# A hybrid two-layer network on one core: another form of the power in the scan step, and the long convolution's transposes and projections issued one group later

## The chip, the core and the metric

The kernel runs on one core of a Trainium2 chip. The core has a matrix engine (TensorE, called PE in the profile), a vector engine (VectorE, DVE), an activation engine (ScalarE, ACT), a general-purpose engine (GpSimd, POOL) and an engine that mostly issues transfers (SyncE, SP). Each has its own queue of instructions; they synchronise through semaphores. The metric is the device time of one execution in microseconds.

## The reference, cut to what matters

The network is a stack of sublayers, each added to x. Two of them are touched. The first is a recurrent scan over 2048 positions of a complex state h (256 channels by 16 modes, for two sequences):

```python
def step(h, inp):
    x_t, dt_t, B_t, C_t, xr_t = inp
    h_carrier = h.mean(axis=1)
    T = jnp.cos((c_phase(xr_t) - c_phase(h_carrier)) / 2.0) ** 2
    alpha = jnp.exp(dt_t[..., None] * A_neg)
    expo = 1.0 + (1.0 - alpha) * KAPPA * (1.0 - T[:, None, :])
    mag, ph = (c_mag(h), c_phase(h))
    cmag = jnp.minimum(jnp.exp(expo * jnp.log(mag + 1e-08)), 10.0)
    h = from_polar(cmag, ph)
    Bx = B_t[:, None, :, :] * (dt_t * x_t)[:, :, None, None]
    h = h + Bx
    h = from_polar(jnp.tanh(c_mag(h)), c_phase(h))
    y_t = jnp.einsum('bnc,bdnc->bd', C_t, h)
    return (h, y_t)
```

So each step raises the magnitude of h to a power that depends on the angle between h's mean over the channels and a given direction, adds an input, and squashes the magnitude with tanh. Step t needs all of step t-1. The second is a sublayer with a short causal convolution of four taps, a Silu, a long causal convolution with 1024 taps for each of 512 channels, a gate and a projection:

```python
xz = jnp.einsum('bld,ed->bel', hidden_states, W_in)
x, z = jnp.split(xz, 2, axis=1)
...
x = _silu(xc)
...
n = 2 * Lq
x_f = jnp.fft.rfft(x, n=n)
k_f = jnp.fft.rfft(k_ssm, n=n)
y = jnp.fft.irfft(x_f * k_f[None], n=n)[..., :Lq]
y = y + x * D_skip[None, :, None]
y = y * _silu(z)
return jnp.einsum('bhl,dh->bld', y, W_out)
```

## The kernel before

**The scan.** The state of a step lies as 128 partitions (two sequences, 16 modes, four quarters of the channels) by two planes (real and imaginary) by 64 channels, in hist. A hardware loop of four turns runs over 32 groups of 16 steps, 2048 steps in all. Inside it the order of every engine's instructions is the order in which the code is written (manual_schedule). In `step` (L388 to L480) the mean over the channels comes first: the last step's sums hs go through eight small matmuls (L400) into two PSUM tiles hc and hd, of which ACT reads hc and DVE reads hd. ACT makes n2c, the squared length of the mean, from hc (L415), then its logarithm and ci, one over its length (L423, L424). DVE makes dot, its product with the given direction, from hd (L417). With lg, the logarithm of the magnitude with its small additions, the power is split in two factors: ea = exp(om lg) (L429, L433) and fac = exp(ci lg dot ng) (L431, L440), where ng and om are prepared from alpha a group ahead by `decay` (L373 to L377). The unit vector p = h times il (L435, L436) is multiplied by ea (L438) and by fac (L443), and bx, the input, is added (L445). The rest of the step makes the magnitude m (L458 to L460), its inverse ir (L462), e = exp(-2m) (L463) and sg = 1/(1+e) (L465, L467), and forms the new h in two DVE operations with sums (L474), each followed by an instruction that reads the sum out into hs. In between and behind them DVE makes t2, the new squared magnitude, out of e2 and s2 of ACT (L479), and y1 (L480), from which the next step's logarithms l2 and lh start (L405, L409). Two hooks, act_gap and dve_gap, place work of other steps: the next step's bx (L381) and a part of `decay` behind fac on ACT; outputs and tables on DVE. `project` (L485) is the output product of the step before, on PE behind the mean. `load` (L355) issues the transfers of the next group on SP.

**The long convolution** (sublayer c). The 512 channels are four blocks e of 128. For each block and each of its 16 groups g of channels, `convolve` (L1156) issues 288 pairs of weight load and matmul on PE against Toeplitz windows of the taps, which `kernels` (L1097) loads three groups ahead at most, 2 x 1216 KB for a group, on SP and ACT. `produce(e, ch)` makes a chunk of 512 positions of the next block: a matmul (L1119), a copy on ACT (L1125), four taps on DVE (L1128, L1130), Silu on ACT into c_xs (L1132), and then at once the transpose on PE (ps_t, L1140) and its copy into the ring c_x on DVE (L1144). `finish(e, ch)` takes a chunk of the block before: it loads yc and xs back on POOL (L1176, L1177), makes the gate by a matmul and Silu (L1181, L1183), multiplies on DVE (L1184, L1185) and at once projects on PE (ps_o, L1189) and adds to x (L1193). Only PE's order is the written one here; the other engines' order comes from the scheduler. Behind the convolution of each even group a finish stands, behind that of each odd group a produce. Ahead of the first block stand eight produces, behind the last one eight finishes.

Of the kernel before, what the change touches and what calls it, by code (L numbers as in the profile page):

```python
# [17 lines left out]
AF = mybir.ActivationFunctionType  # L18
# [5 lines left out]
P = 128  # L24
# [39 lines left out]
class Kernel:  # L64
# [189 lines left out]
    def scan(self, y, dtd, dxd, tabd):  # L254
# [9 lines left out]
        with ExitStack() as c:  # L264
# [51 lines left out]
            with nc.allow_non_contiguous_dma(reason="short vectors"):  # L316
# [15 lines left out]
            t2 = [new(cp, [P, J], f"t2{j}") for j in range(2)]  # L332
            y1 = [new(cp, [P, J], f"y1{j}") for j in range(2)]
            bx = [new(cp, [P, 2, J], f"bx{j}") for j in range(2)]
            tg = [[new(cp, sh, f"{n}{j}") for n, sh in (
                ("tc", [P, 6, TG]), ("ng", [P, TG, J]), ("om", [P, TG, J]), ("dx", [P, TG, J]),
# [6 lines left out]
            V.tensor_tensor(t2[1], first[:, 1], first[:, 1], ALU.mult)  # L343
            V.tensor_tensor(y1[1], first[:, 0], first[:, 0], ALU.mult)
            V.tensor_tensor(t2[1], t2[1], y1[1], ALU.add)
            V.scalar_tensor_tensor(y1[1], first[:, 0], 2.0 * SMALL, t2[1], ALU.mult, ALU.add)
# [3 lines left out]
            def load(t0, j):  # L350
                tc_, ng, om, dx, cs = tg[j]
# [11 lines left out]
            def picked(j, k2):  # L363
                V.tensor_tensor(
                    tg[j][4][:, k2], tg[j][0][:, 2 + k2, :].unsqueeze(2).to_broadcast([P, TG, 8]),
                    pick.rearrange("p b r -> p (b r)").unsqueeze(1).to_broadcast([P, TG, 8]), ALU.mult,
                )

            def decay(j, s0, n, what):

                ng, om = tg[j][1][:, s0 : s0 + n], tg[j][2][:, s0 : s0 + n]
                if what == 0:
                    A.activation(ng, ng, AF.Exp, scale=aneg)  # L373
                elif what == 1:
                    A.activation(om, ng, AF.Identity, scale=-0.125, bias=0.625)
                else:
                    A.activation(ng, ng, AF.Identity, scale=0.125, bias=-0.125)  # L377

            def drive(j, k, k2, o):

                A.activation(  # L381
                    bx[o][:, k2], tg[j][3][:, k], AF.Identity, scale=tg[j][0][:, k2, k : k + 1],
                    bias=0.0 if k2 else SMALL,
                )

            w = lambda sh, name: new(wp, [P, *sh], name)
            wa = lambda name: new(pa, [P, J], name)

            def step(k, g, before, act_gap, dve_gap):

                tc_, ng, om, dx, cs = tg[g]
                ng, om = ng[:, k], om[:, k]
# [4 lines left out]
                hc, hd = new(pp, [P, 2], "hc"), new(pp, [P, 2], "hd")  # L397
# [23 lines left out]
                ln, ci, il = wa("lr")[:, 0:1], w([1], "ci"), w([J], "il")  # L421
                A.activation(il, lh, AF.Exp, scale=-0.5)
                A.activation(ln, n2c, AF.Ln, bias=1e-18)  # L423
                A.activation(ci, ln, AF.Exp, scale=-0.5)  # L424
# [8 lines left out]
                A.activation(ea, a, AF.Exp)  # L433
                p = w([2, J], "p")
                V.scalar_tensor_tensor(p[:, 0], h[:, 0], SMALL, il, ALU.add, ALU.mult)  # L435
                V.tensor_tensor(p[:, 1], h[:, 1], il, ALU.mult)  # L436
                for k2 in range(2):
                    V.tensor_tensor(p[:, k2], p[:, k2], ea, ALU.mult)  # L438
                fac = w([J], "fac")
                A.activation(fac, ngd, AF.Exp, scale=ci)  # L440
# [16 lines left out]
                m, lr = wa("m"), wa("lr")  # L457
                A.activation(m, m2, AF.Ln)  # L458
                A.activation(lr, r1, AF.Ln)
                A.activation(m, m, AF.Exp, scale=0.5)  # L460
# [1204 lines left out]
```

## Time and profile before

| | us |
|---|---|
| median of 3 runs | 14502.04 (14501.18 to 14502.08) |
| the profiled execution | 14511.68 |
| its span in the profile | 14510.0 |
| DVE busy | 10157.4 (70%) |
| ACT busy | 8884.8 (61%) |
| PE busy, weight loads apart | 5471.0 (38%) |
| POOL busy | 419.8 (3%) |
| mean granted PE clock | 0.616 of full speed |

By stage, from the windows of the trace:

| stretch, us | DVE busy | ACT busy | PE busy | granted PE clock | GB/s of DMA |
|---|---|---|---|---|---|
| 0 to 300, ahead of the scan | 213.90 | 108.84 | 155.26 | 0.73 | 51 |
| 5000 to 9000, in the scan | 3303.19 | 3090.32 | 769.64 | 0.50 | 15 |
| 11500 to 12000, in the long convolution | 83.56 | 30.11 | 297.54 | 0.80 | 164 |

How to read it: a group of the profile is one line, engine, operation and shape, with its count, its busy time and the mean duration of one in nanoseconds; behind a bar stands the engine's idle time just ahead of it, and who ended it. A timeline row has the start, the duration and the instruction. The duration of an operation includes its latency; the next one on the same engine can start before it ends. "issue" means that the engine waited for nothing that the profile shows.

### The profile page before, as it was taken

What the parts mean: (1) busy time and instruction counts of PE and PEld (TensorE: products, weight loads), DVE (VectorE), ACT (ScalarE), POOL (GpSimd) and SP (SyncE); (2) the same over time, 40 slices, a digit from 0 to 9 for tenths busy, and PEclk for the clock granted to TensorE, in tenths of its full rate; (3) what the DMA queues carried; (4) which work ended last, traced back from release to release, by engine and by line L of the source; (5) the groups of instructions that cost most, each with busy time, mean ns of one, the idle gap of its engine ahead of it and who ended that gap; (6) DMA issues with size and microseconds to landing.
All of it is one profiled execution on the core that took longest, in us unless ns stands there. A gap on an engine that the chain in (4) does not pass through costs nothing. (4 is left out here: it accounts for less than half of the span.)

```text
span 14510.0 us, 276079 instructions
## 1 busy us (share of the span) xinstructions
PE 5471.0 (38%) x72424; PEld 3825.2 (26%) x72424; DVE 10157.4 (70%) x63112; ACT 8884.8 (61%) x47340; POOL 419.8 (3%) x496
## 2 busy tenths in 40 slices
PE   4111111111111111111111111111797555878889
PEld 1111111111111111111111111111454444544445
DVE  6888888888888888888888888888475111355552
ACT  3777777777777777777777777777162000134442
POOL 0000000000000000000000000000000000121110
PEclk6555555555555555555555555555697787989999
DMA  2000000000000000000000000000001666142210
GB/s 65 13 16 16 13 16 16 16 13 16 16 16 13 16 16 13 16 16 16 13 16 16 15 15 16 16 13 16 25 1 40 166 162 168 29 88 35 35 28 14
DMA packets 349072, 460.71 MB, mean 32 GB/s; under 512 B 204930, under 2 KB 244937, under 8 KB 346452
## 3 DMA queue, kind: packets, MB, share of 16 engines
q1 hardware_dynamic: 296276, 319.90, 9.8%
q10 hardware_dynamic: 36352, 88.61, 2.6%
q0 software_dynamic: 14848, 34.36, 0.8%
q8 instruction: 580, 9.50, 0.3%
q14 instruction: 1016, 8.32, 0.2%
HBM read 385.55 MB, written 52.46 MB: 30 GB/s over the span
## 5 line engine op out<-in xcount | busy, mean ns | idle before, releaser
L400 PE MATMUL hc<-hs,mean 128*32 128x2 f32 x16384 | 588.7, 200 | 7982.7 <-DVE y L480 7727.5
L400 PEld LDWEIGHTS hc<-hs,mean 128*32 128x32 f32 x16384 | 472.7, 140 | 8115.0 <-ACT l L405 8038.0
L470 DVE TENSOR_TENSOR p<-p,ir 128x64 f32<-128x64 f32 x4096 | 739.1, 222 | 1063.4 <-ACT ir L462 1063.4
L485 PE MATMUL yps<-cs,hist 128*64 128x8 f32 x8192 | 1225.3, 259 | 13.8 <-DVE hs L474 13.8
L458 ACT ACTIVATE m<-m 128x64 f32<-128x64 f32 x2048 | 466.2, 228 | 1233.0 <-DVE m L452 1233.0
L381 ACT ACTIVATE bx<-dx,tc 128x64 f32<-128x64 f32 x4098 | 1170.1, 333 | 0.0
L1489 ACT ACTIVATE d_p<-ps_e 128x512 f32<-128x512 f32 (+3 forms) x1280 | 599.6, 537 | 756.0 <-PE ps_o L1470 535.2
L485 PEld LDWEIGHTS yps<-cs,hist 128*64 128x64 f32 x8192 | 1033.5, 218 | 45.9 <-DVE hs L474 14.2
L405 ACT ACTIVATE l<-t 128x64 f32<-128x64 f32 x2048 | 466.2, 228 | 766.2 <-DVE t L479 766.1
L474 DVE CUSTOM_DVE_ANT_0 hist<-p,sg 128x64 f32<-128x64 f32 x4096 | 910.7, 222 | 26.9 <-ACT s L468 6.4
L411 DVE SCALAR_TENSOR_TENSOR lg<-ih,l 128x64 f32<-128x64 f32 x2048 | 454.3, 222 | 561.5 <-ACT ih L407 557.3
L443 DVE TENSOR_TENSOR p<-p,fac 128x64 f32<-128x64 f32 x4096 | 739.9, 222 | 16.7 <-DVE p L438 6.6
L438 DVE TENSOR_TENSOR p<-p,ea 128x64 f32<-128x64 f32 x4096 | 742.0, 222 | 6.0 <-DVE p L438 4.7
L472 DVE SCALAR_TENSOR_TENSOR p<-e,p 128x64 f32<-128x64 f32 x4096 | 739.8, 222 | 6.0 <-ACT sg L467 5.3
L445 DVE TENSOR_TENSOR p<-p,bx 128x64 f32<-128x64 f32 x4096 | 726.1, 219 | 1.4
L440 ACT ACTIVATE fac<-ngd,ci 128x64 f32<-128x64 f32 x2048 | 692.4, 338 | 6.3 <-DVE p L436 5.4
L400 PE MATMUL hd<-hs,mean 128*32 128x2 f32 x16384 | 603.9, 193 | 0.0
L1482 PE MATMUL ps_e<-d_qt,d_kt 128*128 128x512 f32 (+3 forms) x1280 | 556.5, 444 | 44.2 <-ACT d_p L1489 35.6
L431 DVE SCALAR_TENSOR_TENSOR ngd<-lg,dot,ng 128x64 f32<-128x64 f32 x2048 | 570.4, 279 | 0.9 <-DVE a L429 0.9
L1439 PE MATMUL ps_m<-d_kt,d_qt 128*128 128x512 f32 (+3 forms) x1280 | 500.2, 438 | 101.1 <-DVE d_part L1444 41.0
L400 PEld LDWEIGHTS hd<-hs,mean 128*32 128x32 f32 x16384 | 532.7, 157 | 0.0
L1156 PE MATMUL ps_c<-toep,c_x 64*32 64x128 f32 x18432 | 405.6, 335 | 316.3 <-issue 281.4
(429 smaller groups left out, 21285.6 us busy)
## 6 DMA issues: line engine op xcount, KB each, us to landing
toep<-in_C_krev ACTq DMA_DIRECT2D x64, 1216.0 KB, 13.3
toep<-in_C_krev SPq DMA_DIRECT2D x64, 1216.0 KB, 10.7
ng<-dtd SPq DMA_DIRECT2D x258, 256.0 KB, 3.6
dx<-dxd SPq DMA_DIRECT2D x258, 256.0 KB, 4.3
d_kt<-d_kd SPq DMA_DIRECT2D x128, 128.0 KB, 4.4
d_qt<-d_qd SPq DMA_DIRECT2D x128, 128.0 KB, 4.4
y<-ys SPq DMA_DIRECT2D x512, 8.0 KB, 1.9
c_xd<-c_xs POOLq DMA_DIRECT2D x32, 256.0 KB, 7.3
```

What stands on the lines that cost most here:

```text
L381: A.activation(bx[o][:, k2], tg[j][3][:, k], AF.Identity, scale=tg[j][0][:, k2, k : k + 1], bias=0.0 if k2 else SMALL,)
L400: nc.tensor.matmul(out[r : r + 32], mean[:, r : r + 32], hs[i], start=True, stop=True)
L431: V.scalar_tensor_tensor(ngd, lg, dot, ng, ALU.mult, ALU.mult)
L438: V.tensor_tensor(p[:, k2], p[:, k2], ea, ALU.mult)
L440: A.activation(fac, ngd, AF.Exp, scale=ci)
L443: V.tensor_tensor(p[:, k2], p[:, k2], fac, ALU.mult)
L445: V.tensor_tensor(p[:, k2], p[:, k2], bx[o][:, k2], ALU.add)
L470: V.tensor_tensor(p[:, k2], p[:, k2], ir, ALU.mult)
L472: V.scalar_tensor_tensor(p[:, k2], e, -1.0, p[:, k2], ALU.add, ALU.mult)
L474: V.tensor_tensor_reduce(out=hn[:, k2], in0=p[:, k2], in1=sg, scale=-1.0, scalar=0.0 if k2 else J * SMALL, op0=ALU.mult, op1=ALU.add, accu ...
L485: nc.tensor.matmul(yps[:, k, :], hist[g][:, k, k2], tg[g][4][:, k2, k], start=k2 == 0, stop=k2 == 1)
L1489: A.activation(pr[:, q0:], s[:, q0:], AF.Exp, scale=0.25)
```

## The change

In the scan the power is written otherwise. Before, |h|^expo = exp(om lg) exp(ng lg cos) times the unit vector. After, p = h ek fac with fac = exp(lg ng (cos - 1)), so that h itself takes the part of exponent one, and with ek an exponential of the small additions alone. The factor cos - 1 = ci dot - 1 is a new ACT operation on one column, c1, which then is the scale of fac. The carried values of a step are x (minus the magnitude, from e and sg), kc and dl (small additions) instead of t2 and y1; for them ACT makes rm, lb, k1 and k2c. om goes. The tiles hc and hd are made once ahead of the loop, and a matmul of one column with ci is written into hd after its reader. In the convolution the transpose is a function `turn`, called a group later than its produce, and the projection a function `project`, called a group later than its finish; in the prologue and at the end `later` holds them back by one chunk. With om's 8 KB of each partition free, the scheduler places the load of x (L575 before) ahead of the scan.

```diff
-            t2 = [new(cp, [P, J], f"t2{j}") for j in range(2)]
-            y1 = [new(cp, [P, J], f"y1{j}") for j in range(2)]
+            x, kc, dl = ([new(cp, [P, J], f"{n}{j}") for j in range(2)] for n in ("x", "kc", "dl"))
             bx = [new(cp, [P, 2, J], f"bx{j}") for j in range(2)]
             tg = [[new(cp, sh, f"{n}{j}") for n, sh in (
-                ("tc", [P, 6, TG]), ("ng", [P, TG, J]), ("om", [P, TG, J]), ("dx", [P, TG, J]),
+                ("tc", [P, 6, TG]), ("ng", [P, TG, J]), ("dx", [P, TG, J]),
                 ("cs", [P, 2, TG, 8]))] for j in range(2)]
...
-                hc, hd = new(pp, [P, 2], "hc"), new(pp, [P, 2], "hd")
                 for out in (hc, hd):
                     for r in range(0, P, 32):
                         nc.tensor.matmul(out[r : r + 32], mean[:, r : r + 32], hs[i], start=True, stop=True)
                 before()
 
-
-                l2 = wa("l2")
-                A.activation(l2, t2[i], AF.Ln, bias=MAG_EPS)
-                ih = w([J], "ih")
-                A.activation(ih, l2, AF.Exp, scale=-0.5)
-                lh = w([J], "lh")
-                A.activation(lh, y1[i], AF.Ln)
-                lg = w([J], "lg")
-                V.scalar_tensor_tensor(lg, ih, 2.0 * MAG_EPS, l2, ALU.mult, ALU.add)
+                lh, lg, kd = (w([J], n) for n in ("lh", "lg", "kd"))
+                A.activation(lh, x[i], AF.Ln, scale=-1.0)
 
 
                 sq, n2c = w([2], "sq"), w([1], "n2c")
@@ -418,26 +419,25 @@
                     out=junk, in0=hd, in1=tc_[:, 4:6, k], scale=1.0, scalar=0.0, op0=ALU.mult, op1=ALU.add,
                     accum_out=dot,
                 )
-                ln, ci, il = wa("lr")[:, 0:1], w([1], "ci"), w([J], "il")
-                A.activation(il, lh, AF.Exp, scale=-0.5)
+                V.scalar_tensor_tensor(kd, kc[i], 0.5, dl[i], ALU.mult, ALU.add)
+                V.scalar_tensor_tensor(lg, lh, 2.0, kc[i], ALU.mult, ALU.add)
+                ln, ci, c1, ek = wa("lr")[:, 0:1], w([1], "ci"), w([1], "c1"), w([J], "ek")
                 A.activation(ln, n2c, AF.Ln, bias=1e-18)
                 A.activation(ci, ln, AF.Exp, scale=-0.5)
-
-
-
-                a = w([J], "a")
-                V.tensor_tensor(a, om, lg, ALU.mult)
-                ngd = w([J], "ngd")
-                V.scalar_tensor_tensor(ngd, lg, dot, ng, ALU.mult, ALU.mult)
-                ea = w([J], "ea")
-                A.activation(ea, a, AF.Exp)
+                A.activation(ek, kd, AF.Exp)
+                A.activation(c1, ci, AF.Identity, scale=dot, bias=-1.0)
+
+
+                nc.tensor.matmul(hd[32:33, 0:1], ci, self.ident[:, 0:1], start=True, stop=True)
+
+
+                gl = w([J], "gl")
+                V.tensor_tensor(gl, lg, ng, ALU.mult)
                 p = w([2, J], "p")
-                V.scalar_tensor_tensor(p[:, 0], h[:, 0], SMALL, il, ALU.add, ALU.mult)
-                V.tensor_tensor(p[:, 1], h[:, 1], il, ALU.mult)
-                for k2 in range(2):
-                    V.tensor_tensor(p[:, k2], p[:, k2], ea, ALU.mult)
+                V.scalar_tensor_tensor(p[:, 0], h[:, 0], SMALL, ek, ALU.add, ALU.mult)
+                V.tensor_tensor(p[:, 1], h[:, 1], ek, ALU.mult)
                 fac = w([J], "fac")
-                A.activation(fac, ngd, AF.Exp, scale=ci)
+                A.activation(fac, gl, AF.Exp, scale=c1)
...
-                m, lr = wa("m"), wa("lr")
-                A.activation(m, m2, AF.Ln)
+
+
+                lm, m, lr = wa("lm"), wa("m"), wa("lr")
+                A.activation(lm, m2, AF.Ln)
                 A.activation(lr, r1, AF.Ln)
-                A.activation(m, m, AF.Exp, scale=0.5)
-                ir, e, sg, e2, s2 = (w([J], n) for n in ("ir", "e", "sg", "e2", "s2"))
+                A.activation(m, lm, AF.Exp, scale=0.5)
+                ir, e, sg, rm = (w([J], n) for n in ("ir", "e", "sg", "rm"))
                 A.activation(ir, lr, AF.Exp, scale=-0.5)
                 A.activation(e, m, AF.Exp, scale=-2.0)
+                A.activation(rm, lm, AF.Exp, scale=-1.0)
                 le = wa("m")
                 A.activation(le, e, AF.Ln, bias=1.0)
-                A.activation(e2, e, AF.Square, bias=-1.0)
                 A.activation(sg, le, AF.Exp, scale=-1.0)
-                A.activation(s2, le, AF.Exp, scale=-2.0)
+                lb, k1, k2c = wa("lb"), w([J], "k1"), w([J], "k2c")
+                A.activation(lb, m2, AF.Ln, bias=MAG_EPS)
+                A.activation(k1, rm, AF.Ln, scale=MAG_EPS, bias=1.0)
+                A.activation(k2c, lb, AF.Exp, scale=-0.5)
...
-                    if k2 == 0:
-                        V.tensor_tensor(t2[o], e2, s2, ALU.mult)
-                V.scalar_tensor_tensor(y1[o], hn[:, 0], 2.0 * SMALL, t2[o], ALU.mult, ALU.add)
+                V.scalar_tensor_tensor(x[o], e, -1.0, sg, ALU.add, ALU.mult)
+                V.scalar_tensor_tensor(dl[o], hn[:, 0], -SMALL, rm, ALU.mult, ALU.mult)
+                V.scalar_tensor_tensor(kc[o], k2c, 2.0 * MAG_EPS, k1, ALU.mult, ALU.add)
...
+                return e, ch, xs
+
+            def turn(e, ch, xs):
+
+                b, i0 = ch // 4, ch % 4 * 4
...
+                return e, ch, yc
+
+            def project(e, ch, yc):
...
+            due = []
+
+            def later(step, *todo):
+
+                for f, args in due:
+                    f(*args)
+                due[:] = [(step, a) for a in todo]
+
             for ch in range(NCH):
-                produce(0, ch)
+                t = produce(0, ch)
+                later(turn, t)
+            later(turn)
             for e in range(E):
                 for g in range(HALF // 4):
                     t = kernels(e, g)
@@ -1202,12 +1225,19 @@
                     convolve(e, g, t, ps)
                     if g % 4 == 3:
                         leave(e, g - 3, ps)
-                    if g % 2 == 0 and e > 0:
-                        finish(e - 1, g // 2)
-                    if g % 2 == 1 and e + 1 < E:
-                        produce(e + 1, g // 2)
+                    if g % 2 == 0:
+                        work = []
+                        if e + 1 < E:
+                            work.append((turn, produce(e + 1, g // 2)))
+                        if e > 0:
+                            work.append((project, finish(e - 1, g // 2)))
+                    else:
+                        for f, args in work:
+                            f(*args)
             for ch in range(NCH):
-                finish(E - 1, ch)
+                t = finish(E - 1, ch)
+                later(project, t)
+            later(project)
```

The lines left out put `decay` on two passes over 8 steps where it had three over 12, and compute the first x, kc and dl ahead of the loop.

More of the change, by code (lines that the diff above doesn't have):

```diff
@@ L342, in scan @@
             V.tensor_scalar(hs[1][:, 0:1], hs[1][:, 0:1], J * SMALL, None, ALU.add)
[L343 to L346, printed above, removed]
+            n0 = new(wp, [P, J], "lh")
+            A.preload_act_table_set(LOG_EXP)
+            V.tensor_tensor(n0, first[:, 1], first[:, 1], ALU.mult)
+            V.tensor_tensor(kc[1], first[:, 0], first[:, 0], ALU.mult)
+            V.tensor_tensor(n0, n0, kc[1], ALU.add)
+            A.activation(kc[1], n0, AF.Ln, bias=MAG_EPS)
+            A.activation(x[1], kc[1], AF.Exp, scale=-0.5)
+            V.scalar_tensor_tensor(kc[1], x[1], 2.0 * MAG_EPS, kc[1], ALU.mult, ALU.add)
+            A.activation(n0, n0, AF.Ln)
+            V.tensor_tensor(kc[1], kc[1], n0, ALU.subtract)
+            A.activation(x[1], n0, AF.Exp, scale=-1.0)
+            V.scalar_tensor_tensor(dl[1], first[:, 0], -SMALL, x[1], ALU.mult, ALU.mult)
+            A.activation(x[1], n0, AF.Exp, scale=0.5)
+            V.tensor_scalar(x[1], x[1], -1.0, None, ALU.mult)
             yv = y.rearrange("p k (b t) -> p k b t", b=B)
             def load(t0, j):
-                tc_, ng, om, dx, cs = tg[j]
+                tc_, ng, dx, cs = tg[j]
                 for d, t in ((dtd, ng), (dxd, dx)):
@@ L364, in picked @@
                 V.tensor_tensor(
-                    tg[j][4][:, k2], tg[j][0][:, 2 + k2, :].unsqueeze(2).to_broadcast([P, TG, 8]),
+                    tg[j][3][:, k2], tg[j][0][:, 2 + k2, :].unsqueeze(2).to_broadcast([P, TG, 8]),
                     pick.rearrange("p b r -> p (b r)").unsqueeze(1).to_broadcast([P, TG, 8]), ALU.mult,
@@ L369, in decay @@
             def decay(j, s0, n, what):
-                ng, om = tg[j][1][:, s0 : s0 + n], tg[j][2][:, s0 : s0 + n]
+                ng = tg[j][1][:, s0 : s0 + n]
                 if what == 0:
                     A.activation(ng, ng, AF.Exp, scale=aneg)
-                elif what == 1:
-                    A.activation(om, ng, AF.Identity, scale=-0.125, bias=0.625)
                 else:
@@ L381, in drive @@
                 A.activation(
-                    bx[o][:, k2], tg[j][3][:, k], AF.Identity, scale=tg[j][0][:, k2, k : k + 1],
+                    bx[o][:, k2], tg[j][2][:, k], AF.Identity, scale=tg[j][0][:, k2, k : k + 1],
                     bias=0.0 if k2 else SMALL,
                 )
+            hc, hd = new(pp, [P, 2], "hc"), new(pp, [P, 2], "hd")
             w = lambda sh, name: new(wp, [P, *sh], name)
@@ L389, in step @@
             def step(k, g, before, act_gap, dve_gap):
-                tc_, ng, om, dx, cs = tg[g]
-                ng, om = ng[:, k], om[:, k]
+                tc_, ng, dx, cs = tg[g]
+                ng = ng[:, k]
                 h = hist[g][:, k - 1] if k else hist[1 - g][:, TG - 1]
@@ L485, in project @@
                     nc.tensor.matmul(
-                        yps[:, k, :], hist[g][:, k, k2], tg[g][4][:, k2, k], start=k2 == 0, stop=k2 == 1
+                        yps[:, k, :], hist[g][:, k, k2], tg[g][3][:, k2, k], start=k2 == 0, stop=k2 == 1
                     )
@@ L502, in scan @@
                 drive(0, 0, k, 0)
-            for what in range(3):
+            for what in range(2):
                 decay(0, 0, TG, what)
@@ L521, in act_gap @@
                                 rows(iv + (g + 1) * TG, nxt)
-                            if 3 <= k < 15:
-                                decay(nxt, (k - 3) // 3 * 4, 4, k % 3)
+                            if 3 <= k < 11:
+                                decay(nxt, (k - 3) // 2 * 4, 4, (k - 3) % 2)
                         def dve_gap(k):
```

## The prediction

> **What bounds the kernel now.** I read the windows first. The scan (0.365 to 10.178 ms) is 9813 of the 14510 us of the span, with VectorE (DVE) busy 83% and ScalarE (ACT) 77% of it: neither is full, so it is bound by a chain. The chain of waits names only the last 2% of the span, so I read one scan step in the timeline instead; all steps there repeat at 4.75 us (5000.35 to 5005.10). Columns: start, duration, engine, line, operation, out<-in, [idle before <- what ended it].
>
> ```profile
> 5000.35 0.23 DVE L474 CUSTOM_DVE_ANT_0 hist<-p,sg 128x64 f32<-128x64 f32 x1
> 5000.51 0.08 DVE L474 DVE_READ_ACCUMULATOR2_ANT hs<- 128x1 f32 x1
> 5000.51 0.22 DVE L479 TENSOR_TENSOR t<-e,s 128x64 f32<-128x64 f32 x1
> 5000.64 0.22 DVE L474 CUSTOM_DVE_ANT_0 hist<-p,sg 128x64 f32<-128x64 f32 x1
> ...
> 5000.79 0.08 DVE L474 DVE_READ_ACCUMULATOR2_ANT hs<- 128x1 f32 x1
> ...
> 5001.02 0.29 PE L400 MATMUL hc<-hs,mean 128*32 128x2 f32 x8 [3.83 <-DVE y L480]
> ...
> 5001.36 0.17 ACT L415 ACTIVATE sq<-hc 128x2 f32<-128x2 f32 x1
> 5001.43 0.20 ACT L415 ACTIVATION_READ_ACCUMULATOR sq<-hc 128x1 f32 x1
> ...
> 5001.67 0.16 ACT L423 ACTIVATE lr<-n2c 128x1 f32<-128x1 f32 x1
> ...
> 5001.86 0.17 ACT L424 ACTIVATE ci<-lr 128x1 f32<-128x1 f32 x1
> ...
> 5001.93 0.25 ACT L433 ACTIVATE ea<-a 128x64 f32<-128x64 f32 x1
> ...
> 5002.08 0.34 ACT L440 ACTIVATE fac<-ngd,ci 128x64 f32<-128x64 f32 x1
> 5002.21 0.36 DVE L438 TENSOR_TENSOR p<-p,ea 128x64 f32<-128x64 f32 x2
> ...
> 5002.54 0.36 DVE L443 TENSOR_TENSOR p<-p,fac 128x64 f32<-128x64 f32 x2
> ...
> 5003.75 0.23 ACT L458 ACTIVATE m<-m 128x64 f32<-128x64 f32 x1 [0.55 <-DVE m L452]
> ```
>
> From here on stamps are cut to their last digits (2.42 is 5002.42). With the first hist at T: sum of h read out by T+0.52, TensorE (PE) mean T+0.67, sq T+1.01, ci T+1.51, fac T+1.73, p times fac T+2.19, m T+3.40, next hist T+4.75. Two chains run side by side up to p times fac: hs, mean, sq, n2c, ci, fac (ACT), ending at 2.42; and DVE's row of multiplies, whose first p<-p,ea ends at 2.43. The start at 2.54 follows DVE's end by 0.11, the gap that p<-e,p also shows behind p<-p,ir (4.63 to 4.74), where DVE's own result is the later of two waits. Where ACT's is the later, the gap is 0.03 (ea ends 2.18, p<-p,ea starts 2.21).
>
> **Scan, part by part.** DVE loses a, the two p<-p,ea, t2, y1 and gains kd, x, dl, kc; ngd (279 ns) becomes gl. ACT loses l2, ih, il, e2, s2 and the om pass (512 of 400 ns), and gains ek, c1, rm, lb, k1, k2c. These counts matter little: DVE idles 0.27 + 0.56 us in a step and ACT's lb, k1, k2c follow sg, where ACT waited 0.37 us. The chain decides:
>
> 1. hs. t2 stood between the two hist operations (0.51 to 0.64). Without it the second starts with the first one's read: -0.13. x, dl, kc come behind hs. Bound: if the second must await the first's 0.08 read, only -0.05. I take -0.13, because t2 and y, too, start at the same stamp as the read.
> 2. PE. Its first mean matmul waited for DVE and ACT; a one-column matmul on ci now takes the ACT wait early, and the built listing leaves DVE alone. From the read's end (0.87) to the weight load (0.98) is 0.11, again the two-wait gap; one wait costs 0.05 to 0.06 (dot read ends 1.63, ngd starts 1.69). -0.055; bounds 0 and -0.06. Nothing is queued behind the new matmul but the next step's means; it needs ci, half a step before hs.
> 3. sq to ci: il between them goes, and it delayed nothing (1.52 + 0.15). -0.005. lh, which stands ahead of sq, waits for x: ends T+0.53, lh starts T+0.57, sq may follow 0.15 later, before hc is there (T+0.78).
> 4. **c1** is new on the chain: fac needs c1, which needs ci. Before, fac started ci + 0.22, with ea in between. Now ek stands there and c1 starts ci + 0.22; fac follows its end by 0.035. No row shows a one-column ACT operation with a scale from memory. From rows: one-column Exp, SBUF to SBUF (aneg, L327) 202 ns; a scale from memory adds 90 ns (fac 338 against ea 248; 493 against 400 at 256 columns): 0.29. The Trainium skill (ScalarE: Activation LUTs, What ACT_TABLE_LOAD costs) prices it at 186 + 0.833 N ns and about 93 for a pointer operand: 0.28, the rule that speaks against the change; the 12 ns between them are 25 us over 2048 steps, the row is taken. +0.325; lower bound +0.235, if the scale's fetch runs ahead.
> 5. p times fac. DVE's side is now done early: ek ends ci + 0.32, the first p is ready at ci + 0.58; fac ends ci + 0.88. It starts 0.035 behind fac, where 0.12 lay before: -0.085.
> 6. From there to m, 1.21: unchanged. Then sg: without e2 ahead, 0.05 earlier (4.78), but hist also awaits p<-e,p: -0.015, bounds 0 and -0.03.
>
> Sum: -0.13 -0.055 -0.005 +0.325 -0.085 -0.015 = **+0.035 us a step**, times 2048 = +72 us. The once-only set-up hides in 21 us in which ACT awaits the tables. SP now loads x (8 x 512 KB) before the scan instead of behind it; in front, DMA's share is 0.21 over the first 300 us and DVE is busy 214 of them, and behind the scan PE did not wait for x: 0.
>
> **Convolution** (11.141 to 12.382 ms). PE works in written order; the turns ps_t wait for copy, taps and Silu of the same chunk:
>
> ```profile
> 11632.76 1.98 PE L1140 MATMUL ps_t<-ident,c_xs 128*64 128x64 f32 x32 [4.28 <-ACT c_xs L1132]
> 11634.67 4.83 PE L1156 MATMUL ps_c<-toep,c_x 64*32 64x128 f32 x188
> 11642.80 3.04 PE L1156 MATMUL ps_c<-toep,c_x 64*32 64x128 f32 x100 [3.30 <-issue]
> ...
> 11649.21 1.10 PE L1189 MATMUL ps_o<-w_C_W_outT,c_yc 128*128 128x256 f32 x4 [1.46 <-issue]
> ```
>
> Waits for c_xs: 138.3 us over 32 turns. Eight lie in the prologue, where seven now find the next chunk's matmul ahead: 7 x 4.33 = -30. Of the first ps_o of each finish (1.48 each), 7 of the 8 at the end go: -10. The other 24 turns (104 us) and 24 ps_o (36 us) lie among convolutions, whose own waits are called "issue", 281 us. Those come after runs of 128 matmuls (128 more weight loads), and the instruction queue moved 154 packets, 2.52 MB: one packet per 256 instructions. So PE stands without instructions while kernels (2 x 1216 KB) load. The skill (Runtime: NRT & Kernel Launch, Instruction fetch mechanics) holds refills in 16 KiB blocks to be mostly hidden; this trace differs with waits of 1.4 to 6.7 us. By the rule both waits go whole, -140; by the rows fetch takes most back: pairs of groups with both waits take 36.6 us (11496.71 to 11679.70, five), those with the first alone 32.7 (11241.25 to 11470.05, seven), those of the last block, without the first, 30.9 (12098.04 to 12283.49, six). Single pairs of each kind show the idle sums 8.8 + 6.6, 10.8 + 4.3 and 12.0 + 2.3 (issue, then named waits): 15.4, 15.1 and 14.3, nearly the same. I take 3.1 off 16 pairs, 2.2 off 8, 0.5 off 8: -71; bounds 0 and -140. Three stalls of 11 us at block changes (DVE's copies behind a c_yc that awaits its load) go, as the listing puts the copies first; fetch ran ahead in them: -15, bounds 0 and -32. The turns' copies (420 ns each) and the additions to x (688) move along and lie beside a DVE busy some 15%. DMAs on SP and ACT keep their places; on POOL only reads of xs and yc shift, with two buffers each. Together **-126**.
>
> **Total**: 14511.7 (the profiled run; span 14510.0) + 72 - 126 = 14458. That run lies 9.6 us above the median of the runs, so I forecast 14448. Less than 0.2% (29 us) cannot be told from no change.
>
> **Rivals.**
> - *c1 costs less*: scale fetched ahead (-0.09 a step), sg's full -0.03. Step -0.07, -143 - 126: 14233 to 14350. For it: duration rows say little on when a pointer is read; against: both sizes pay 90 ns in full. 0.21.
> - *Fetch takes all back in the pairs*: -40 in the convolution, +72: 14534. For it: idle sums hardly fall with fewer waits; against: they fall a little. 0.14.
> - *Slower by the accumulator*: the second hist holds until the first one's sum is read, +0.08 a step (+164): 14612. It decides from +0.06 us a step (126/2048) upward. For it: no row has two such operations in sequence; against: t2 and y never waited. PE's wait not falling adds 113 more. 0.20.
> - That the change does not do what it says: the listing shows the waits moved; 0 beyond the cases above.
>
> **Numbers.** Forecast 0.45, own range 14390 to 14510. Faster: 0.38 of it and 0.21; within 0.2%: 0.05 and 0.07; slower: the rest. Range 14300 to 14630: half of the first rival and half of the third lie outside.
>
> **What would show it.** One c1 row near 290 ns between ci and fac; hist's second start 0.16 behind the first; PE's weight load 0.05 behind the read; p<-p,fac released by ACT; step 4.785. In the convolution no wait for c_xs above 1 us, "issue" above 281, blocks' pairs near 33. I am wrong if the step moves by over 0.06 us, or if the pairs keep 36 us.

## The result, and the profile after

The changed kernel took **14362.76 us** (median of 4 runs, 14356.83 to 14365.42) beside 14502.06 for the kernel before (4 runs, 14501.18 to 14503.2): ratio **0.9903, 95% interval 0.9886 to 0.992**, 139 us less. The forecast was 14448, which is 54 less: the fall is 2.6 times the forecast one. The time lies in the prediction's whole range (14300 to 14630), but below the range of its forecast alone (14390 to 14510). The profiled execution took 14364.49 us, its span 14362.8.

By stage, from the instructions that begin and end each (us of the span):

| stage | before | after | difference | forecast |
|---|---|---|---|---|
| ahead of the scan | 366.0 | 364.5 | -1.5 | 0 |
| scan | 9812.7 | 9824.0 | **+11.3** | +72 |
| scan to the convolution's first matmul | 962.5 | 959.2 | -3.3 | 0 |
| convolution | 1247.6 | 1094.2 | **-153.4** | -126 |
| rest | 2121.2 | 2120.9 | -0.3 | 0 |

DVE's busy time went from 10157.4 to 9934.6 us, ACT's from 8884.8 to 9106.3, PE's from 5471.0 to 5808.5 (the one-column matmuls).

First the scan: the timeline of the changed kernel, with the end of one step and the first half of the next, in the same columns as in the prediction.

```profile
5008.77 0.23 DVE L479 CUSTOM_DVE_ANT_0 hist<-p,sg 128x64 f32<-128x64 f32 x1
...
5008.92 0.08 DVE L479 DVE_READ_ACCUMULATOR2_ANT hs<- 128x1 f32 x1
5008.92 0.22 DVE L479 CUSTOM_DVE_ANT_0 hist<-p,sg 128x64 f32<-128x64 f32 x1
5009.07 0.08 DVE L479 DVE_READ_ACCUMULATOR2_ANT hs<- 128x1 f32 x1
...
5009.20 0.20 PEld L408 LDWEIGHTS hc<-hs,mean 128*32 128x32 f32 x8 [3.60 <-DVE hs L479]
...
5009.56 0.17 ACT L416 ACTIVATE sq<-hc 128x2 f32<-128x2 f32 x1
...
5010.06 0.17 ACT L426 ACTIVATE ci<-lr 128x1 f32<-128x1 f32 x1
...
5010.28 0.29 ACT L428 ACTIVATE c<-ci,dot 128x1 f32<-128x1 f32 x1
...
5010.59 0.35 ACT L440 ACTIVATE fac<-gl,c 128x64 f32<-128x64 f32 x1
...
5010.98 0.36 DVE L443 TENSOR_TENSOR p<-p,fac 128x64 f32<-128x64 f32 x2 [0.20 <-ACT fac L440]
```

With the first hist again at T: the second follows at T + 0.15 (before + 0.29) and starts at the stamp of the first one's read, not behind it. PE loads weights 0.05 after the second read (T + 0.30 + 0.08), where it was 0.11, and its idle time is now ended by DVE's hs. sq stands at T + 0.79 (1.01), ci at 1.29 (1.51): 0.22 won. Then c1 takes it back: fac starts ci + 0.53 (ci + 0.22). What follows fac by 0.04 is p times fac, at T + 2.21 (2.19), with ACT as the one waited for. All told the step is nearly where it was: steps without a stall (within 0.05 us of the median step) take 4.765 us in the mean, against 4.751.

Then the convolution: a pair of groups in PE's timeline of the changed kernel, and PE's prologue as the windows view gives it for before and after (stretch, its length, busy time and count of PE, PE's weight loads, DVE, ACT, POOL, the granted PE clock, DMA's share, GB/s).

```profile
11470.82 2.09 PE L1124 MATMUL ps<-c_xT,w_C_W_inT 128*128 128x512 f32 x4
11472.75 1.88 PE L1191 MATMUL ps<-c_xT,w_C_W_inT 128*128 128x512 f32 x4
11474.56 3.46 PE L1166 MATMUL ps_c<-toep,c_x 64*32 64x128 f32 x229
11483.82 1.95 PE L1166 MATMUL ps_c<-toep,c_x 64*32 64x128 f32 x59 [5.79 <-issue]
11485.69 1.97 PE L1150 MATMUL ps_t<-ident,c_xs 128*64 128x64 f32 x32
11487.60 1.39 PE L1202 MATMUL ps_o<-w_C_W_outT,c_yc 128*128 128x256 f32 x4
```

```profile
11141.00:11220.00 79.00, 43.87 (x288) 23.57 (x288) 28.17 (x55) 11.18 (x18) 4.52 (x8) 0.65 0.07 28
```

```profile
11147.70:11187.50 39.80, 29.64 (x288) 16.49 (x288) 26.72 (x56) 11.00 (x17) 4.51 (x8) 0.84 0.13 54
```

Neither ps_t nor the first ps_o waits any more; in the same pair the convolution's matmuls wait 5.79 for "issue". The prologue halves: its idle time falls from 35.1 to 10.2 us, and the same 288 matmuls are busy 29.64 us instead of 43.87, at a granted clock of 0.84 instead of 0.65. One row of the prologue before and one after show it:

```profile
11170.72 3.78 PE L1119 MATMUL ps<-c_xT,w_C_W_inT 128*128 128x512 f32 x4
```

```profile
11162.60 1.98 PE L1124 MATMUL ps<-c_xT,w_C_W_inT 128*128 128x512 f32 x4
```

In the waits view (us in total, times, longest) PE shows after

```profile
PE ps_c L1166 <- issue: 382.7, 87, 6.7
PE ps_t L1150 <- ACT c_xs L1137: 9.6, 5, 2.6
```

where before had

```profile
PE ps_c L1156 <- issue: 281.4, 95, 6.7
PE ps_t L1140 <- ACT c_xs L1132: 138.3, 32, 4.8
```

129 us of named waits went, and 101 came back as "issue". The five waits for c_xs that are left are in the prologue and last 1.6 to 2.6 us; the prediction had named none above 1 us.

### The profile page after: what moved, and what is told of

Its sections match the earlier page's. It is cut to its first block, busy times and chain, and to the rows that moved or that the text cites. A ratio compares the mean times of both kernels' runs of the same rounds, so it can differ in the third digit from the quotient of the medians.

```text
span 14362.8 us, 279683 instructions
## 1 busy us (share of the span) xinstructions
PE 5808.5 (40%) x76520; PEld 3905.5 (27%) x76520; DVE 9934.6 (69%) x61067; ACT 9106.3 (63%) x46835; POOL 418.8 (3%) x496
## 5 line engine op out<-in xcount | busy, mean ns | idle before, releaser
L408 PEld LDWEIGHTS hc<-hs,mean 128*32 128x32 f32 x16384 | 410.5, 140 | 7462.8 <-DVE hs L479 7398.0
L460 ACT ACTIVATE lm<-m 128x64 f32<-128x64 f32 x2048 | 466.2, 228 | 1179.7 <-DVE m L452 1179.7
L412 ACT ACTIVATE lh<-x 128x64 f32<-128x64 f32 x2048 | 525.2, 256 | 551.1 <-DVE x L483 551.0
L479 DVE CUSTOM_DVE_ANT_0 hist<-p,sg 128x64 f32<-128x64 f32 x4096 | 764.0, 223 | 23.5 <-ACT lb L471 5.1
L440 ACT ACTIVATE fac<-gl,c 128x64 f32<-128x64 f32 x2048 | 712.3, 348 | 68.9 <-DVE p L437 3.0
L428 ACT ACTIVATE c<-ci,dot 128x1 f32<-128x1 f32 x2048 | 584.2, 285 | 0.0
L1512 PE MATMUL ps_e<-d_qt,d_kt 128*128 128x512 f32 (+3 forms) x1280 | 556.7, 444 | 43.9 <-ACT d_p L1519 35.5
L1166 PE MATMUL ps_c<-toep,c_x 64*32 64x128 f32 x18432 | 386.0, 321 | 383.8 <-issue 382.7
L1469 PE MATMUL ps_m<-d_kt,d_qt 128*128 128x512 f32 (+3 forms) x1280 | 501.3, 438 | 97.4 <-DVE d_part L1474 37.6
L408 PE MATMUL hd<-hs,mean 128*32 128x2 f32 x16384 | 539.7, 193 | 0.0
L431 PE MATMUL hd<-ident,ci 128*1 128x1 f32 x4096 | 386.9, 164 | 358.8 <-ACT ci L426 358.8
L1479 DVE TENSOR_REDUCE d_part<-ps_m 128x1 f32<-128x512 f32 x768 | 494.7, 683 | 41.7 <-PE ps_m L1469 41.1
L437 DVE SCALAR_TENSOR_TENSOR p<-hist,ek 128x64 f32<-128x64 f32 x2048 | 460.8, 225 | 84.5 <-ACT ek L427 0.9
```

Source lines behind the costliest of these rows:

```text
L408: nc.tensor.matmul(out[r : r + 32], mean[:, r : r + 32], hs[i], start=True, stop=True)
L428: A.activation(c1, ci, AF.Identity, scale=dot, bias=-1.0)
L440: A.activation(fac, gl, AF.Exp, scale=c1)
L479: V.tensor_tensor_reduce(out=hn[:, k2], in0=p[:, k2], in1=sg, scale=-1.0, scalar=0.0 if k2 else J * SMALL, op0=ALU.mult, op1=ALU.add, accu ...
L1512: nc.tensor.matmul(s[:, q0:], ks[kt // 4][:, hh, kt % 4 * P : (kt % 4 + 1) * P], q[:, hh, q0:], start=True, stop=not diag,)
```

## The experiments

Every run stands beside runs of the kernel before on its own chip, whose median lay between 14501 and 14524. So the table gives the difference to that median, and, where a run is the changed kernel with one edit, the difference of the differences, taken from after's -139.3; divided by 2048 it is the price in a scan step.

| run | median | minus before | ratio to before, interval | against after | a step |
|---|---|---|---|---|---|
| scan changed alone | 14523.14 | +12.8 | 1.001 (1.0003 to 1.0017) | | +0.006 |
| convolution changed alone | 14350.22 | -160.1 | 0.9892 (0.9877 to 0.9907) | | |
| no one-column matmul | 14531.92 | +21.6 | 1.0017 (1.0009 to 1.0025) | +160.9 | +0.079 |
| x between the hists | 14636.19 | +126.0 | 1.0086 (1.0073 to 1.01) | +265.3 | +0.130 |
| c1 without pointer | 14180.82 | -329.5 | 0.9776 (0.9763 to 0.979) | -190.2 | -0.093 |
| old scan, one-column matmul, new convolution | 14308.27 | -193.0 | 0.9867 (0.9852 to 0.9882) | | |
| c1 on DVE | 14335.02 | -166.3 | 0.9884 (0.9869 to 0.9899) | -27.0 | -0.013 |
| ci in PSUM | 14455.75 | -45.5 | 0.9968 (0.9956 to 0.998) | +93.8 | +0.046 |
| c1 on DVE, ln apart | 14229.2 | -281.0 | 0.9805 (0.9791 to 0.9818) | -141.7 | -0.069 |
| kernels loaded once | 13985.69 | -515.6 | 0.9645 (0.963 to 0.9659) | -376.3 | |
| one load queue | 14435.55 | -74.7 | 0.9946 (0.9932 to 0.9959) | +64.6 | |
| turns later only | 14439.38 | -84.4 | 0.994 (0.9926 to 0.9953) | +54.9 | |

### Each half alone

Theory: the scan's changes nearly cancel, and the whole gain is the convolution's. Rival: one half helps the other (clock, alignment of the instruction fetch). The edits are the diff's parts as they stand, the scan's in one run and the convolution's in the other.

> The changed scan with the convolution as it was before. If the traces are read rightly, the scan costs +11.3 us of the span (9812.7 to 9824.0): about 14511 us (14505 to 14520), within 0.2% of before. The prediction's own sum (+0.035 us a step) would give 14574.

> The changed convolution with the scan as it was before. If the traces are read rightly, the whole gain is here: 14502 - 153 = 14349 us (14340 to 14360). The prediction's own sum (-126) would give 14376. If part of the -153 came only through the new scan (another clock, another alignment of the instruction fetch), it stays nearer to 14376.

+12.8 and -160.1, close to what the traces gave, and their sum of -147.3 is 8 us from the -139.3 of both together; before's own medians differ by up to 22.5 us. Within that spread the halves are independent, and the prediction's scan sum (+72) is refuted.

### What the one-column matmul is worth

```diff
-                nc.tensor.matmul(hd[32:33, 0:1], ci, self.ident[:, 0:1], start=True, stop=True)
```

> The changed kernel without the one-column matmul on ci, so that the first mean matmul again waits for two engines. Theory: the second wait costs what the prediction took, 0.055 us a step: 14363 + 113 = 14476. If the whole 0.09 us by which sq now follows the hist operations sooner (beyond the hist part) hangs on it: 14363 + 184 = 14547. Rival: the wait for ACT is long met by then and costs nothing: 14363, and the weight load follows the read by 0.05 us all the same.

+160.9, 0.079 us a step: between the two sizes of the theory, nearer to the larger, and the rival is out. The end of a step in that run's timeline:

```profile
5006.46 0.21 ACT L472 ACTIVATE k2c<-lb 128x64 f32<-128x64 f32 x1
...
5006.68 0.08 DVE L478 DVE_READ_ACCUMULATOR2_ANT hs<- 128x1 f32 x1
...
5006.88 0.23 PEld L408 LDWEIGHTS hc<-hs,mean 128*32 128x32 f32 x7 [3.99 <-ACT k2c L472]
5006.91 0.29 PE L408 MATMUL hc<-hs,mean 128*32 128x2 f32 x8 [3.92 <-DVE x L482]
...
5007.25 0.17 ACT L416 ACTIVATE sq<-hc 128x2 f32<-128x2 f32 x1
```

The last ACT operation named, k2c, ends at 6.67, before the read of hs ends at 6.76, so the wait for ACT was met; all the same the weight load starts 0.12 behind the read instead of 0.05, the matmul another 0.03 behind its weight load instead of at the same stamp, and sq stands at T + 0.87 instead of T + 0.79. The label behind "<-" names an engine that PE was not held by.

The packed traces show what held it. They also list semaphore instructions, which the views leave out. In before and in this run the first mean weight load itself waits for ACT, and the wait for DVE is an instruction of its own ahead of it in PE's queue; the weight load starts 0.025 behind the end of that instruction. In after the one-column matmul has this pair of waits, and the mean's weight load waits for DVE alone. So what counts is which event comes last. p times fac in after has a separate wait for DVE ahead of it as well, but ACT's fac comes last there, and it starts only 0.03 to 0.04 behind fac.

This run beside the one with the convolution alone also gives the power's new form without the matmul: 21.6 + 160.1 = +181.7 us, 0.089 a step.

Would the old step have had the same from it? The matmul, with hc and hd made once, was put into the scan of before, beside the changed convolution:

```diff
+            hc, hd = new(pp, [P, 2], "hc"), new(pp, [P, 2], "hd")
...
-                hc, hd = new(pp, [P, 2], "hc"), new(pp, [P, 2], "hd")
...
                 A.activation(ci, ln, AF.Exp, scale=-0.5)
+                nc.tensor.matmul(hd[32:33, 0:1], ci, self.ident[:, 0:1], start=True, stop=True)
```

> The scan as before plus the one-column matmul on ci (hc and hd made once), with the changed convolution; the run with the changed convolution alone was at 14350. Theory: the early wait is worth as much in the old step, since both of its chains (dot, ngd, DVE's multiplies; n2c, ci, fac) begin at the mean matmul: -0.05 to -0.08 us a step (DVE's lg, which ends just ahead of junk, is late next), 14186 to 14248. That would make the power's new form itself slower than the old one. Rival: DVE's row of multiplies up to p<-p,ea is bound by a and ea, which await no matmul: 0 to -40, 14310 to 14350.

-193.0 + 160.1 = -32.9, 0.016 a step: the rival's range. The profiled executions of these two runs differ by 56 us in the scan, 0.027 a step, somewhat above that range; either size is far below the theory's 0.05 to 0.08. Why the theory fails is seen in rows of that run (first hist at 5002.02):

```profile
5002.94 0.22 DVE L411 SCALAR_TENSOR_TENSOR lg<-ih,l 128x64 f32<-128x64 f32 x1 [0.27 <-ACT ih L407]
...
5003.07 0.15 DVE L417 CUSTOM_DVE_ANT_0 junk<-hd,tc 128x2 f32<-128x2 f32 x1
...
5003.19 0.22 DVE L430 TENSOR_TENSOR a<-om,lg 128x64 f32<-128x64 f32 x1
```

sq is sooner by 0.09 (T + 0.92), but lg stands at T + 0.92 where it was at 0.93: it hangs on t2, l2 and ih, not on the mean. The row of DVE's operations behind lg moves up 0.03 only. The new form, in which lg needs x and kc alone, is what lets the matmul pay.

### The other terms of the step

Both runs price one term of the prediction's sum. x back between the two hist operations, where t2 had stood:

```diff
-                V.scalar_tensor_tensor(x[o], e, -1.0, sg, ALU.add, ALU.mult)
+                    if k2 == 0:
+                        V.scalar_tensor_tensor(x[o], e, -1.0, sg, ALU.add, ALU.mult)
```

> The changed kernel with x put between the two hist operations, where t2 stood before. Theory: every operation in that place delays the second hist, its sum and the mean by 0.13 us, all of it on the chain: 14363 + 0.13 x 2048 = 14363 + 266 = 14629 (14600 to 14640). Rival: the second sum has slack (lh, which needs x, is late instead): x comes 0.15 us sooner and ScalarE's lh with it, so that less than half remains, up to 14490.

+265.3, or 0.130 a step: theory, to the digit.

c1 with a constant for its scale:

```diff
-                A.activation(c1, ci, AF.Identity, scale=dot, bias=-1.0)
+                A.activation(c1, ci, AF.Identity, scale=0.001, bias=-1.0)
```

> The changed kernel with c1 scaled by a constant instead of dot (the cosine is left out of the power, all instructions stay). Theory: a scale read from memory costs 0.09 us of c1, and c1 is on the chain: 14363 - 184 = 14179, c1 rows near 195 ns. Rival: the pointer is read ahead or c1 is not on the chain (DVE's multiplies of h would be late next, by a gap of 0.11): 14363, or down to no more than -0.05 us a step, 14260.

-190.2. In its timeline c1 is 0.19 us long and fac starts 0.23 behind it:

```profile
5004.42 0.17 ACT L426 ACTIVATE ci<-lr 128x1 f32<-128x1 f32 x1
...
5004.63 0.19 ACT L428 ACTIVATE c<-ci 128x1 f32<-128x1 f32 x1
...
5004.86 0.35 ACT L440 ACTIVATE fac<-gl,c 128x64 f32<-128x64 f32 x1
```

With the pointer c1 takes 285 ns in the mean of its 2048, and all 0.09 us of the difference reach the end. That settles the first rival of the prediction (a scale fetched ahead): it isn't.

### Versions that might beat both

If c1 is on the chain, its place can be cheaper. On DVE, between gl and the first product:

```diff
-                A.activation(c1, ci, AF.Identity, scale=dot, bias=-1.0)
...
                 V.tensor_tensor(gl, lg, ng, ALU.mult)
+                V.tensor_scalar(c1, ci, dot, -1.0, ALU.mult, ALU.add)
```

> The changed kernel with c1 = ci dot - 1 made by VectorE between gl and the first product with h, instead of by ScalarE. Theory: c1 is on the chain, and a one-column DVE operation takes about 0.16 us plus 0.06 for its operand from memory, 0.04 after ci and 0.03 ahead of fac: fac starts about ci + 0.45 instead of ci + 0.54 (sum 0.17 + 0.04 + 0.21 + 0.03), -0.09 us a step, 14363 - 184 = 14179. Rival: the products with h, which it pushes back by 0.14 us, become late, or each crossing costs 0.11 instead of 0.03: no gain, 14363 or some 100 more.

Only -27. The first half did what was expected (c1 206 ns in the mean, fac at ci + 0.47, 0.06 less), so neither the theory nor its rival was right: 0.05 was lost behind it. The rows of the second half:

```profile
5001.43 0.21 DVE L454 SCALAR_TENSOR_TENSOR r<-q 128x64 f32<-128x64 f32 x1
5001.54 0.23 ACT L460 ACTIVATE lm<-m 128x64 f32<-128x64 f32 x1 [0.45 <-DVE m L452]
5001.73 0.23 ACT L461 ACTIVATE lr<-r 128x64 f32<-128x64 f32 x1
5001.90 0.18 ACT L462 ACTIVATE m<-lm 128x64 f32<-128x64 f32 x1
```

lr starts 0.09 after r ends (0.06 in the changed kernel), and m, which ACT issues behind it, lm + 0.36 instead of lm + 0.31. In this run's trace lr has come to wait for two: it waits for its own engine, and a semaphore instruction that waits for DVE (r1) stands ahead of it. The tile lr is also read by ci, and the older wait of ACT's that covered this read, that of c1, is gone. In the changed kernel ACT's only such pair in a step is at fac. So the logarithm ahead of ci was put into another tile:

```diff
-                ln, ci, c1, ek = wa("lr")[:, 0:1], w([1], "ci"), w([1], "c1"), w([J], "ek")
+                ln, ci, c1, ek = wa("lb")[:, 0:1], w([1], "ci"), w([1], "c1"), w([J], "ek")
```

> c1 on VectorE, as in the run at 14335, and the logarithm ahead of ci written into lb's tile instead of lr's. In that run lr came to wait for VectorE and for its own engine (ci's read of the tile, which c1 on ScalarE used to cover), lr started lm + 0.19 instead of + 0.17 and hist lm + 1.41 instead of + 1.36. Theory: it is the second wait, as it was for TensorE; with a tile of its own lr follows r by 0.06 again, and -0.05 us a step comes back: 14335 - 100 = 14235 (14215 to 14250). Rival: the half behind p times fac is longer for another reason (z, q and the products start in another phase): 14335.

-141.7, of which -114.7 (0.056 a step; 0.050 by the scans of the two traces) is this one name. ACT has no such pair of waits left in an ordinary step, and in the timeline the gaps are back:

```profile
5004.94 0.22 DVE L454 SCALAR_TENSOR_TENSOR r<-q 128x64 f32<-128x64 f32 x1
5005.06 0.23 ACT L460 ACTIVATE lm<-m 128x64 f32<-128x64 f32 x1 [0.36 <-DVE m L452]
5005.22 0.21 ACT L461 ACTIVATE lr<-r 128x64 f32<-128x64 f32 x1
5005.37 0.18 ACT L462 ACTIVATE m<-lm 128x64 f32<-128x64 f32 x1
```

It is the fastest version here that computes the whole: **14229.2 us, 0.9805 of before (0.9791 to 0.9818)**, against 0.9903 for the change.

The other way tried was ci in PSUM, c1 ahead of ek:

```diff
-                ln, ci, c1, ek = wa("lr")[:, 0:1], w([1], "ci"), w([1], "c1"), w([J], "ek")
+                lc, ek = wa("lr"), w([J], "ek")
+                ln, ci, c1 = lc[:, 0:1], lc[:, 1:2], w([1], "c1")
...
+                A.activation(c1, ci, AF.Identity, scale=dot, bias=-1.0)
                 A.activation(ek, kd, AF.Exp)
-                A.activation(c1, ci, AF.Identity, scale=dot, bias=-1.0)
-                nc.tensor.matmul(hd[32:33, 0:1], ci, self.ident[:, 0:1], start=True, stop=True)
+                nc.tensor.matmul(hd[32:33, 0:1], n2c, self.ident[:, 0:1], start=True, stop=True)
```

> The changed kernel with ci in PSUM, c1 ahead of ek on ScalarE, and the one-column matmul fed from n2c. Theory: what comes from PSUM reaches the next ScalarE operation sooner (rows: m to m in PSUM 178 ns, SBUF to SBUF 248), and ek no longer stands between: -0.03 to -0.06 us a step, 14240 to 14300. Rival: c1 starts no sooner than ci's end plus the same gap, and ek, which is now behind c1, delays the products with h: 14363 to 14460.

+93.8: the rival. fac does start sooner (ci + 0.49), but ek, now behind c1, holds the products with h, and p times fac stands at T + 2.24 instead of 2.21. It starts 0.12 behind fac (5002.35 to 5002.47) and no longer 0.04, because DVE's own product (5002.37) is again the later of its two waits.

```profile
5001.86 0.25 ACT L429 ACTIVATE ek<-kd 128x64 f32<-128x64 f32 x1
5002.01 0.34 ACT L441 ACTIVATE fac<-gl,c 128x64 f32<-128x64 f32 x1
5002.14 0.23 DVE L438 SCALAR_TENSOR_TENSOR p<-hist,ek 128x64 f32<-128x64 f32 x1 [0.32 <-ACT ek L429]
...
5002.47 0.36 DVE L444 TENSOR_TENSOR p<-p,fac 128x64 f32<-128x64 f32 x2
```

### The convolution: who holds PE up

The prediction read "issue" as instruction fetch that stands behind the kernels' loads. To tell it from a slowness of the fetch itself, three tiles are loaded once and used for all groups:

```diff
+            held = []
...
-                t = new(kb, [P, 4, W], "toep")
+                if len(held) == 3:
+                    return held[g % 3]
+                t = new(kp, [P, 4, W], f"toep{g}")
+                held.append(t)
```

> The changed kernel with the kernels' tiles of the first three groups of the convolution loaded once and used for all groups (so its output is not the reference's; 61 of the 64 pairs of loads of 2 x 1216 KB are gone). Theory: TensorE's issue waits in the convolution (383 us) are its instruction fetch kept waiting by these loads: they fall by more than half, and the convolution by 150 us or more, to 14210 or less. Rival: the fetch itself is as slow without other traffic (or these waits are something else in TensorE): issue stays at 350 to 390 and the time within 20 us of 14363.

-376.3, and the waits view of that run has

```profile
PE ps_c L1171 <- issue: 115.4, 83, 2.4
```

The windows view for a long stretch of the changed kernel's convolution, then of this run's:

```profile
11260.00:12220.00 960.00, 577.32 (x17954) 429.91 (x17954) 156.87 (x265) 60.31 (x103) 51.25 (x84) 0.79 0.74 180
```

```profile
11250.00:11850.00 600.00, 461.40 (x17341) 337.98 (x17342) 159.63 (x268) 60.21 (x103) 52.76 (x85) 0.97 0.17 54
```

Nearly as many matmuls take 600 us instead of 960, with DMA's share at 0.17 instead of 0.74. 267 us of issue waits are gone, and PE is busy 461 instead of 577, at a granted clock of 0.97 instead of 0.79. From the convolution's first own matmul to its last it is 621.5 us instead of 998.6: 257 less idle and 120 less busy. The loads cost this convolution more than the change won. The rest of the issue waits, 115 us, is there without them. They were not waits for the tiles themselves: they come between the 229th and the 230th matmul of one group, whose first matmuls have used both halves of its tile long before. Their places speak for the fetch: of the waits over 0.9 us, 82 in after and 72 in this run, each stands a multiple of 256 PE instructions (to within 4) behind the one before, and 256 is what the prediction counted for one packet of the instruction queue.

Would one load queue beside the fetch be better than two?

```diff
-                    (nc.scalar if r else nc.sync).dma_start(
+                    nc.sync.dma_start(
```

> The changed kernel with both halves of each kernel load of the convolution issued from SyncE's queue, none from ScalarE's. With these loads gone TensorE's issue waits fell from 382.7 to 115.4 us. Theory: the instruction fetch shares the 16 engines with the queues that have packets, so with one load queue instead of two it is served sooner: issue falls to 250 to 320, 14363 - 60 to - 130 = 14230 to 14300. Rival: what counts is the bytes in flight (DMA's share stays near 0.74), 14363 within 20; or one queue is too slow for 2 x 1216 KB in a group's 15 us, then TensorE waits for toep itself and the time is above 14363.

+64.6, in none of the ways named: the issue waits rise.

```profile
PE ps_c L1166 <- issue: 437.2, 86, 7.5
```

PE does not wait for toep, and DMA's share is 0.77, its rate 172 GB/s. What makes the fetch wait longer behind one queue stays open.

Last, the two parts of the convolution's change. The turns stay a group later; a finish projects its chunk at once:

```diff
-                            work.append((project, finish(e - 1, g // 2)))
+                            project(*finish(e - 1, g // 2))
...
-                t = finish(E - 1, ch)
-                later(project, t)
-            later(project)
+                project(*finish(E - 1, ch))
```

> The changed kernel with only the convolution's turns a group later; finish projects its chunk at once, as before (64 of 64 ps_o pairs, those of the epilogue too). Theory by the prediction's terms: the projections' share is 0.9 us in each of 16 pairs of groups, 0.5 in each of the last 8 and 10 in the epilogue, 28 us: 14363 + 28 = 14391; by the traces of before and after rather more (pairs 1.2 in 16, epilogue 16): 14400. Rival: the fetch takes the projections' waits back as well, only the epilogue's stay: 14373 to 14379.

+54.9: more than the theory by either of its counts, and the rival is far off. The first ps_o of a pair in that run, with the work of DVE and ACT that it needs:

```profile
11495.30 1.98 PE L1124 MATMUL ps<-c_xT,w_C_W_inT 128*128 128x512 f32 x4
11497.12 1.88 PE L1191 MATMUL ps<-c_xT,w_C_W_inT 128*128 128x512 f32 x4
11498.53 2.33 DVE L1135 SCALAR_TENSOR_TENSOR c_acc<-c_xi,w_C_conv_w,c_acc 128x512 f32<-128x512 f32 x3
11499.04 0.60 ACT L1193 ACTIVATE c_acc<-ps 128x512 f32<-128x512 f32 x1 [1.13 <-PE ps L1191]
11500.77 0.75 DVE L1194 SCALAR_TENSOR_TENSOR c_yc<-c_xs,w_C_D_skip,c_yc 128x512 f32<-128x512 f32 x1
11501.62 0.69 DVE L1195 TENSOR_TENSOR c_yc<-c_yc,c_acc 128x512 f32<-128x512 f32 x1
11502.41 1.10 PE L1202 MATMUL ps_o<-w_C_W_outT,c_yc 128*128 128x256 f32 x4 [3.41 <-issue]
```

From the first finish to the 17th, sixteen pairs take 37.6 us each before, 35.5 here and 32.9 after: the projections' share is 2.6 a pair, not 0.9. ps_o's issue waits are 72.7 us in 30 places here, 2.4 each, against 44.4 before, 1.5 each. The label hides what they are. In the body the first ps_o of a finish starts 0.05 to 0.10 behind the end of DVE's last product (L1195), here and before, so it waits for that product and not for instructions. Before, the last product follows finish's Silu by 0.03. Here it follows by 1.5 to 2.3 in the 16 pairs that have a produce too, since with the new order DVE makes produce's taps (L1135) first; the Silu starts 0.04 behind its matmul all the same. So the prediction took the projection's wait as it was in the old order (1.5), and beside the moved produce it is 2.9 to 3.8. The turns' share, with the scan's +12.8 taken off, is -84.4 - 12.8 = -97 us.

## Why the prediction was right, and where its sizes were off

The direction and the chain of reasons held, and the time fell inside the whole range; the sum was 85 us short. The scan makes 61 of it, the convolution 27 and the other stages 5; 8 go off again, since after's profiled run lies nearer to its median than before's (1.7 us above it, against 9.6).

The scan, term by term:

- *hs*, -0.13 a step: the trace has -0.14, the run with x between the hists 0.130. The rival in which the second hist waits for the first one's read is out.
- *PE*, **-0.055, the term that was mis-sized: 0.079** by the run without the matmul. The prediction priced the second wait by the start of the weight load alone (0.11 against 0.05); the matmul itself starts another 0.03 behind its weight load when both wait, and that was in the trace of before too (0.98 and 1.02). 0.024 x 2048 is 49 of the 61 us.
- *c1*, +0.325: 0.31 in the trace (fac at ci + 0.53, before ci + 0.22), and the run with a constant scale shows the pointer's 0.09 in full. Of the two prices that were weighed, 0.29 from the rows and 0.28 from the rule (the Trainium skill, ScalarE: Activation LUTs, What ACT_TABLE_LOAD costs), 285 ns was measured.
- *p times fac*, -0.085: ACT's fac now ends the wait, and the gap behind it is 0.03 to 0.04, as said.
- *sg*, -0.015: nothing. It stands 0.05 sooner behind lm, but hist comes at lm + 1.36 as before: it waits for DVE's product p<-e,p as well, and starts 0.14 behind the end of that in both traces.

With PE's and sg's terms corrected the sum is -0.13 - 0.079 - 0.005 + 0.325 - 0.085 = +0.026 a step, or +0.011 with 0.31 for c1; steps without a stall are +0.014 apart, the mean step over the scan +0.0055 (11.3 / 2048). The last 0.009 are stalls: 171 steps after, and 255 before, take over 0.05 us more than the median, together 65 and 84 us more. DVE has 2051 instructions fewer in the scan (55674 instead of 57725); whether this is the reason was not tried.

The convolution: the forecast of -126 was all idle time, and PE's idle time fell by 109 (540.4 to 431.3, the stage less its busy time). The fetch took back 101 of the waits, which is the prediction's main point there and held: by waits alone (129 for c_xs, 49 of ps_o's, 33 at the block changes) 211 would have gone. **What the sum left out is PE's busy time**, which fell from 707.2 to 662.9 for the same matmuls, -44: 14 in the prologue, 29 in the body, 1 in the epilogue. In the prologue the rows show where: four ps matmuls 3.78 us before and 1.98 after, with the granted clock at 0.65 and 0.84. The Trainium skill has the rule (TensorE: Matmul & The Clock Gate, Part 1: The HAM clock gate), that the default state is throttled and activity releases it; had the prediction set it beside the waits of 4.3 us, it would have asked what PE does between them. In the body the granted clock is the same (0.79 and 0.78). Some 20 of its 29 us are the convolution's own matmuls (405.5 to 386.0 us busy); where they come from stays open.

By parts: the turns brought -97 where the terms said -98; the projections -55 where they said -28, with 2.6 a pair for 0.9, because produce, now just ahead of finish, had made the wait that they end longer.

## What to carry to other kernels

Where an instruction of the scan step had two waits, the one for DVE was an instruction of its own ahead of it; where DVE's event came last, this cost the step 0.079 us on PE and 0.056 on ACT, though the other wait was long met. On a chain that repeats thousands of times, let an earlier instruction of the same queue take the second wait, and after each edit look in the listing for waits that have grown (a shared temporary is enough). Such a gain counts only if no other chain of the step is as long: the same matmul was worth 161 us in the new step and 33 to 56 in the old.

When waits of an engine disappear, ask what else it was short of, here instructions, and what its clock does when it stops less: the first took back 101 us; with the second, the prologue's matmuls took 14 us less. And price a wait in the new order, not in the old one: work moved ahead of it can make it longer, as produce did with the projections.

## What the runs showed of the hardware that was not expected

- The price of a second wait, on two engines, where the event of the separate wait comes last: PE 0.079 us a step (read to weight load 0.12 instead of 0.05, weight load to matmul 0.03 instead of 0), ACT 0.056 (lr 0.09 behind r instead of 0.06, m lm + 0.36 instead of + 0.31).
- Without 61 of 64 pairs of the kernels' loads the granted clock of PE in the convolution is 0.97 instead of 0.79: the loads cost twice, 257 us of idle time and 120 of busy time for the same matmuls. Whether the clock follows the stops or the loads themselves, no run separates.
- The "issue" waits over 0.9 us of the convolution's own matmuls stand at multiples of 256 PE instructions (to within 4), also when the loads are gone (115 us are left). Not every "issue" is one: the first ps_o of a finish waited for DVE.
- The same bytes from one queue instead of two made PE's issue waits longer (437 us instead of 383), at nearly the same DMA share (0.77 and 0.74).
